# Attention logits by VectorE instead of TensorE, and a shared node tile kept as dense products, in a two-front relational GNN kernel

## The chip, the cores and the metric

The kernel runs on one core of one Trainium2 chip. The metric is device time in microseconds (us) of one execution, median over several runs. A profiled execution gives the trace; its own time is stated beside its span.

## The reference

A graph of 6250 nodes with 256 features and 100000 edges, sorted by destination; each edge has one of 8 relations. Three relational layers are followed by a residual LayerNorm, an attention step and a second residual LayerNorm. Cut to what matters:

```python
for l in range(3):                                   # relational layers
    xr  = einsum('nd,rde->rne', x, W_rel[l])         # 8 products per node
    agg = segment_sum(xr[edge_type, src], dst, N)    # gather by edge, sum by destination
    x   = relu(agg + x @ W_root[l] + bias[l])
x = layernorm(x_in + x)
xt      = (x @ weight).reshape(N, 4, 64)             # attention
alpha_l = einsum('ehd,hd->eh', xt[src], attn_l)      # only edges e < N are used
alpha_r = einsum('ehd,hd->eh', xt[dst], attn_r)
alpha   = softmax(leaky_relu(alpha_l + alpha_r, 0.01))
tmp     = einsum('nh,nhd->nd', alpha[:N], xt[dst[:N]])
out     = layernorm(x + tile(tmp, 4))
```

Everything is float32. `alpha_l` of a node is its normed row times a 256x4 matrix, `weight` folded with `attn_l`; the kernel computes that matrix once (`fold_weights`, columns `D + H` to `D + 2H` of the tile `w1x`).

## The kernel before

**Layers.** Edges are cut in 782 tiles of 128. The first 36 ("hot" ones, of the first few nodes) are handled by counts (`count`, `products`); the other 746 are gathered one by one in each of the three layers. `gather` (L497) has GpSimd issue one indirect DMA per edge tile, 128 rows of 256 floats into a quarter of an `msg` buffer. The pool `mp` has eight such buffers of four tiles, and the hot products and the attention's preparation take buffers from the same pool. `windows` (L514) multiplies the gathered rows with one-hot matrices `oh` (made by VectorE, L481) on TensorE into PSUM, and `add` (L526) has VectorE add the result into a ring `S`, in which the columns of a few node tiles of 128 nodes lie, by relation.

**Two fronts.** The tiles are cut in 188 groups of up to four. Two fronts go down the sorted edges at once and alternate group by group: the upper front (f = 0, ring of 4 node tiles) and the lower one (f = 1, ring of 3). When the last group that touches node tile j of a front is done, `dense` multiplies that tile's `S` with the layer's weights: 2 products with `wo` (L578) and 16 with `wr` (L582), each of which is two float32 passes in the profile. It is a generator: at most six products per group and waiting tile are issued between `windows` and `add`, so they fill in on TensorE. `finish` (L594 to L618) adds the bias, and in layers 0 and 1 applies ReLU and stores the row block for the next layer; in layer 2 it adds the residual and norms the rows to `yt`. `clear` zeroes the columns of the ring on ScalarE (L591).

**The shared tile.** One node tile, number 13, is touched by both fronts. When the lower front is through with it (after group 7) `keep` copies its whole `S` block, 128x2048 floats, to `hold` on ScalarE (L568). After group 181, when the upper front is through, VectorE adds that block to the upper `S` (L825, 128x2048), and one dense product does both.

**Logits.** In layer 2, two groups after a tile is normed, `logits` (L619 to L632) computes its four `alpha_l`: two transposes on TensorE (L549, in `turn`), a copy to SBUF by ScalarE (L552), matmuls with the folded columns (L630) and a copy of 128x4 by VectorE to `altab` (L632). Tile 0 is only transposed, for the attention. From group 164 on `prepare` makes the tables of the attention step between the groups.

**Order.** Within a layer the instructions run on every engine in the order in which the program writes them. Per group: hot products or preparation, loads of rows, `gather`, the one-hot of four groups ahead, `logits` of tiles normed two groups ago, `finish` of the tiles whose products are done, `windows`, the next pieces of `dense`, `add`, transposes of rows (`turn`), then the folding of the ring's end (`fold`, L558 and L560, where a ring wraps) and the queueing of tiles that became ready.

Of the kernel before, what the change touches and what calls it, by code (L numbers as in the profile page):

```python
# [20 lines left out]
P = 128  # L21
# [137 lines left out]
def fast(tc, const, pl, x, xs, src, dst, edge_type, w_rel, w_root, bias, weight,  # L159
# [10 lines left out]
    with ExitStack() as top:  # L170
        tab = top.enter_context(tc.tile_pool(name="tab", bufs=1))
        ident = tab.tile([P, P], F32, name="ident")
        idx = tab.tile([P, CH * P], I32, name="idx")
        key = tab.tile([P, CH * P], F32, name="key")
        pos = tab.tile([1, CH * P], I32, name="pos")
        iota_p = tab.tile([P, 1], F32, name="iota_p")
        eps = tab.tile([P, 1], F32, name="eps")
        bias_b = tab.tile([P, L, D], F32, name="bias_b")
        w1x = tab.tile([P, KC, D + 2 * H], F32, name="w1x")
        altab = tab.tile([P, NT, H], F32, name="altab")  # L180
        al3 = tab.tile([P, 3, NT, H], BF16, name="al3")
        ga = tab.tile([P, NT, H], F32, name="ga")
        hif = tab.tile([P, NT], F32, name="hif")
        dt = tab.tile([P, NT], F32, name="dt")
        yT0 = tab.tile([P, KC, P], F32, name="yT0")


        A = tab.tile([P, NT, HOT * R], F32, name="A")

        psi = top.enter_context(tc.tile_pool(name="psi", bufs=1, space=PSUM))  # L190
        iota = psi.tile([P, max(R * WMAX, NT * R)], F32, name="iota")
        hk = tab.tile([P, pl.TH], F32, name="hk")
        hl = tab.tile([P, pl.TH], F32, name="hl")

        dram = top.enter_context(tc.tile_pool(name="lanes", bufs=1, space=DRAM))
        lane = dram.tile([NT * P], I32, name="lane")
        with tc.tile_pool(name="ps_p", bufs=2, space=PSUM) as ps_p:
            tables(tc, pl, ps_p, src, dst, edge_type, ident, idx, key, pos, iota, iota_p,
                   lane, hk, hl, hif, dt, flag, R, H)
        y = dram.tile([NT * P, D], F32, name="y")  # L200

        with ExitStack() as s:
            wp = s.enter_context(tc.tile_pool(name="wp", bufs=1))
            sp = s.enter_context(tc.tile_pool(name="sp", bufs=1))
            mp = s.enter_context(tc.tile_pool(name="mp", bufs=8))
            op = s.enter_context(tc.tile_pool(name="op", bufs=AHEAD + 2))
            xp = s.enter_context(tc.tile_pool(name="xp", bufs=3))
            hp = s.enter_context(tc.tile_pool(name="hp", bufs=1))
            ps_w = s.enter_context(tc.tile_pool(name="ps_w", bufs=4, space=PSUM))
            ps_d = s.enter_context(tc.tile_pool(name="ps_d", bufs=2, space=PSUM))  # L210
            ps_t = s.enter_context(tc.tile_pool(name="ps_t", bufs=1, space=PSUM))


            S = [sp.tile([P, KR, n * P + PAD], F32, name=f"S{f}") for f, n in enumerate(NS)]

            hold = {j: sp.tile([P, KR, P], F32, name=f"hold{j}") for j in sorted(pl.shared(pl.TM))}

            nc.vector.memset(eps, EPS)
            for t in S:
                nc.scalar.memzero(t)  # L220
            nc.sync.dma_start(bias_b, bias.rearrange("l d -> (l d)").partition_broadcast(P))
            fold_weights(tc, mp, w1x, weight, attn_l, attn_r)

            def load_w(l):
                wr = wp.tile([P, KC, R, D], F32, name="wr")
                wo = wp.tile([P, KC, D], F32, name="wo")
                for k in range(KC):
                    nc.scalar.dma_start(
                        wr[:, k], w_rel[l, :, k * P:(k + 1) * P, :].rearrange("r p e -> p r e"))
                    nc.scalar.dma_start(wo[:, k], w_root[l, k * P:(k + 1) * P, :])  # L230
                return wr, wo

            groups = pl.order()

            ready = {}
            for i, (f, g) in enumerate(groups):
                for j in pl.reach(g):
                    ready[f, j] = i

            with tc.manual_schedule():  # L240
                for l in range(L):
                    wr, wo = load_w(l)
                    opn = layer(
                        tc, pl, l, l == L - 1, groups, ready, S, hold, A, hk, hl, idx, key, pos,
                        iota, ident, wr, wo, bias_b, x, xs, eps, w1x, altab, y,
                        (al3, ga, hif, yT0, lane, dst, iota_p),
                        mp, op, xp, hp, ps_w, ps_d, ps_t, H)

        with tc.manual_schedule():
            attention(tc, pl, opn, A, al3, ga, hif, dt, yT0, iota, ident, eps, w1x, altab, y, out, H)  # L250
# [210 lines left out]
def layer(tc, pl, l, final, groups, ready, S, hold, A, hk, hl, idx, key, pos, iota, ident, wr, wo,  # L461
# [101 lines left out]
        at = (j % NS[f]) * P  # L563
        return S[f][:, :, at:at + P]

    def keep(j):

        i = nc.scalar.copy(hold[j], cols(1, j))  # L568
        tc.add_to_no_dep_group(f"used{l}_1_{j}", i.ins)
        done[1].append(j)  # L570
        clear(1, j)

    def dense(f, j, xT):

        pd = ps_d.tile([P, 512], F32, name="pd")
        s = cols(f, j)
        for k in range(KC):
            nc.tensor.matmul(pd[:, :D], xT[:, k], wo[:, k], start=(k == 0), stop=False)  # L578
            yield
        for k in range(KC):  # L580
            for r in range(R):
                i = nc.tensor.matmul(pd[:, :D], s[:, k * R + r], wr[:, k, r],  # L582
                                     start=False, stop=(k == KC - 1 and r == R - 1))
                tc.add_to_no_dep_group(f"used{l}_{f}_{j}", i.ins)
                if k < KC - 1 or r < R - 1:
                    yield
        done[f].append(j)
        fin.append((f, j, pd))
# [2 lines left out]
        i = nc.scalar.memzero(cols(f, j))  # L591
        tc.add_to_no_dep_group(f"used{l}_{f}_{j}", i.ins)

    def finish(j, pd):  # L594
        n = rows(j)
        nc.vector.tensor_tensor(pd[:, :D], pd[:, :D], bias_b[:, l], ALU.add)  # L596
        if not final:
            h = xp.tile([P, D], F32, name="h", bufs=2)
            nc.scalar.activation(h, pd[:, :D], AF.Relu)  # L599
            nc.sync.dma_start(xs[l + 1][j * P:j * P + n, :], h[:n])  # L600
            return
        xin = xp.tile([P, D], F32, name="xres", bufs=2)
        if n < P:
            nc.vector.memset(xin, 0.0)
        nc.sync.dma_start(xin[:n], x[j * P:j * P + n, :])
        z = xp.tile([P, D], F32, name="h", bufs=2)
        nc.vector.scalar_tensor_tensor(z, pd[:, :D], 0.0, xin, op0=ALU.max, op1=ALU.add)
        st = xp.tile([P, 6], F32, name="st")
        mv = xp.tile([P, 2], F32, name="mv")
        rs = xp.tile([P, 1], F32, name="rs")  # L610
        nc.vector.bn_stats(st, z)
        nc.vector.bn_aggr(mv, st)  # L612
        nc.scalar.activation(rs, mv[:, 1:2], AF.Sqrt, bias=eps)  # L613
        nc.vector.reciprocal(rs, rs)
        yt = xp.tile([P, D], F32, name="yt", bufs=2)
        nc.vector.tensor_scalar(yt, z, mv[:, 0:1], rs, op0=ALU.subtract, op1=ALU.mult)
        nc.sync.dma_start(y[j * P:(j + 1) * P, :], yt)
        return yt  # L618

    def logits(j, yt):  # L620

        if j == 0:
            turn(yt, yT0)
            return
        if prepared:
            opn.append(j)
        yT = turn(yt)
        pt = ps_t.tile([P, 4 * P], F32, name="pt")
        for k in range(KC):
            nc.tensor.matmul(pt[:, :H], yT[:, k], w1x[:, k, D + H:D + 2 * H],  # L630
                             start=(k == 0), stop=(k == KC - 1))
        nc.vector.tensor_copy(altab[:, j], pt[:, :H])  # L632

    def count():

# [140 lines left out]
    prep = prepare() if final else iter(())  # L776
    if final:
        nc.vector.memset(altab, 0.0)
    for i in range(NG + 5):

        ahead = i >= PREP_AT and (i >= NG or groups[i][0] == 1)
# [3 lines left out]
            next(counting, None)  # L785
        if i >= HOT_AT:
            next(hot, None)
        for j in sorted(fetch.get(i, []), reverse=True):
            held[j] = load_rows(j)
        if i < NG:  # L790
# [5 lines left out]
            logits(j, yt)  # L796
        log = [(k, t) for k, t in log if k > i - 2]
        for f, j, pd in fin:
            yt = finish(j, pd)
            clear(f, j)  # L800
            if final:
                log.append((i, (j, yt)))
        fin.clear()
        if i < NG:
# [13 lines left out]
            xTs[j] = turn(held.pop(j))  # L818
        for f, j in sorted((k for k, r in ready.items() if r == i), key=lambda k: -k[1]):
            fold(f, j)  # L820
            if f == 1 and j in late:
                keep(j)
                continue
            if j in hold:
                nc.vector.tensor_tensor(cols(f, j), cols(f, j), hold[j], ALU.add)  # L825
            turned.append(dense(f, j, xTs.pop(j)))
    assert not (turned or fin or log or held or xTs)
    assert next(counting, None) is None and next(hot, 0) == 0 and next(prep, None) is None
    return sorted(opn)
# [544 lines left out]
```

## Time and profile before

| what | value |
|---|---|
| median of 3 runs | 2976.59 us (2976.0 to 2979.49) |
| profiled execution | 2982.89 us, span 2981.1 us |
| mean granted TensorE clock | 0.936 |
| TensorE busy | 2671.0 us (90%) |
| VectorE busy | 1668.5 us (56%) |
| ScalarE busy | 458.6 us (15%) |
| GpSimd busy | 2140.4 us (72%) |
| L497 gathers | 2238, mean 952 ns |
| L549 transposes of `yt`, layer 2 | 98 |
| L630 matmul instructions, layer 2 | 192, mean 266 ns |
| L825 add of the held block | 3, 2291 ns each |

The span runs from the first to the last instruction; the execution's own time also has what lies before and after. Busy time is the share in which an engine executes an instruction; issuing, semaphores and branches don't count. In the views, PE is TensorE, PEld its weight loads, DVE VectorE, ACT ScalarE, POOL GpSimd, SP the engine that only issues DMAs. In a group's row the times after the second bar are the engine's idle time just before these instructions and what ended most of it.

### The profile page before, as it was taken

How to read it: one execution, taken by the hardware profiler on the slowest of the kernel's cores; microseconds unless marked ns; L12 is line 12 of the kernel's file. 1: busy time of each engine (PE TensorE's matmuls, PEld its weight loads, DVE VectorE, ACT ScalarE, POOL GpSimd, SP SyncE). 2: the span in 40 equal slices, each digit the busy share in tenths (PEclk: the TensorE clock that was granted, in tenths of full speed). 3: DMA queues.
4: the chain of work that ended last, by engine and by line, in shares of the span. 5: the costliest groups of instructions: out<-in, count | busy, mean ns of one | idle time of the engine just before them, and what ended most of it. 6: DMA issues, size and time to landing. Idle time of an engine off the chain costs nothing.

```text
span 2981.1 us, 45287 instructions
## 1 busy us (share of the span) xinstructions
PE 2671.0 (90%) x15710; PEld 2428.2 (81%) x15711; DVE 1668.5 (56%) x4094; ACT 458.6 (15%) x602; POOL 2140.4 (72%) x2254
## 2 busy tenths in 40 slices
PE   5999999999877799999988998689999999999985
PEld 4989888888776688988887887678888888888874
DVE  7645677764433455554444443256566655554778
ACT  2111111111001011111111110111111111110114
POOL 6777777777775777777777777577777777777741
PEclk9999999999988899999999997789999999998985
DMA  4444344445433444444444543344444444454534
GB/s 153 125 122 122 119 123 120 120 134 158 146 117 106 122 125 122 125 124 118 120 119 142 170 125 118 117 119 128 130 127 130 123 129 127 133 177 135 165 119 166
DMA packets 203053, 388.97 MB, mean 130 GB/s; under 512 B 42885, under 2 KB 128004, under 8 KB 202820
## 3 DMA queue, kind: packets, MB, share of 16 engines
q0 software_dynamic: 107424, 293.48, 33.6%
q1 hardware_dynamic: 87464, 85.04, 8.8%
q10 hardware_dynamic: 7932, 7.48, 0.8%
q8 instruction: 130, 2.13, 0.3%
q14 instruction: 103, 0.84, 0.1%
HBM read 360.18 MB, written 25.65 MB: 129 GB/s over the span
## 4 chain that ended last, share of the span: by engine, by line
PE 69%; POOL 10%; issue 8%; DVE 6%; DMA 5%; ACT 2%; DVEq 0%; ACTq 0%; POOLq 0%; SPq 0%
PE pw L514 31%; PE pd L582 29%; POOL msg L497 10%; PE pd L578 4%; DMA msg<-x,idx 3%; DVE S L526 3%; PE pd L686 1%; DMA msg<-in_x_dram,idx 1%; PE pt L549 1%; PE pt L630 1%; ACT xT L552 1%; PE pd L657 1%; ACT o L1053 0%; DMA wr<-in_L_gnn_W_rel_dram 0%; DVE oh L481 0%
## 5 line engine op out<-in xcount | busy, mean ns | idle before, releaser
L497 POOL DMA_INDIRECT msg<-x,idx x1492 | 1419.7, 952 | 513.9 <-issue 413.7
L514 PE MATMUL pw<-oh,msg 128*128 128x160 f32 (+22 forms) x8952 | 1305.7, 303 | 202.8 <-DMA msg<-x,idx 99.8
L514 PEld LDWEIGHTS pw<-oh,msg 128*128 128x128 f32 x8952 | 1250.9, 202 | 268.2 <-issue 127.8
L526 DVE TENSOR_TENSOR S<-S,pw 128x320 f32 (+22 forms) x2238 | 905.3, 405 | 998.1 <-PE pd L582 509.0
L582 PE MATMUL pd<-wr,S 128*128 128x256 f32 x4704 | 1108.8, 386 | 1.7 <-DVE S L526 1.4
L582 PEld LDWEIGHTS pd<-wr,S 128*128 128x128 f32 x4704 | 896.3, 194 | 118.0 <-DVE S L526 3.6
L497 POOL DMA_INDIRECT msg<-in_x_dram,idx x746 | 709.2, 951 | 236.1 <-issue 208.4
L481 DVE TENSOR_TENSOR oh<-iota,key 128x640 f32<-128x640 f32 (+23 forms) x564 | 364.2, 647 | 26.5 <-issue 14.8
L591 ACT ACTIVATE S<-S 128x2048 uint32<-128x2048 uint32 x150 | 285.0, 1900 | 0.1
L552 ACT COPY xT<-pt 128x256 f32<-128x256 f32 x195 | 72.3, 371 | 983.6 <-PE pt L549 983.5
L599 ACT ACTIVATE h<-pd 128x256 f32<-128x256 f32 x98 | 37.6, 384 | 933.5 <-DVE pd L596 752.3
L578 PE MATMUL pd<-wo,xT 128*128 128x256 f32 x588 | 170.0, 415 | 3.3 <-ACT h L599 3.3
L596 DVE TENSOR_TENSOR pd<-pd,bias_b 128x256 f32<-128x256 f32 x147 | 63.2, 430 | 172.5 <-PE pd L582 172.5
L578 PEld LDWEIGHTS pd<-wo,xT 128*128 128x128 f32 x588 | 111.2, 207 | 13.3 <-ACT h L599 3.7
L648 DVE TENSOR_SCALAR sel<-iota,hk 128x392 bf16<-128x392 f32 x138 | 80.4, 613 | 0.0
L613 ACT ACTIVATE rs<-mv,eps 128x1 f32<-128x1 f32 x49 | 14.4, 295 | 417.9 <-DVE mv L612 417.9
L686 PE MATMUL pd<-msg,A 128*128 128x256 f32 x294 | 72.5, 390 | 1.5 <-DMA msg<-x 1.5
L686 PEld LDWEIGHTS pd<-msg,A 128*128 128x128 f32 x294 | 56.7, 200 | 8.7 <-issue 1.9
L549 PE MATMUL pt<-ident,xin 128*128 128x128 f32 x294 | 57.6, 278 | 1.4 <-ACT xT L552 1.4
L630 PEld LDWEIGHTS pt<-w1x,xT 128*128 128x128 f32 x192 | 26.6, 201 | 35.2 <-ACT xT L552 35.2
L549 PEld LDWEIGHTS pt<-ident,xin 128*128 128x128 f32 x294 | 41.6, 146 | 12.9 <-ACT xT L552 2.6
L630 PE MATMUL pt<-w1x,xT 128*128 128x4 f32 x192 | 30.8, 266 | 23.5 <-ACT xT L552 23.5
(187 smaller groups left out, 640.0 us busy)
## 6 DMA issues: line engine op xcount, KB each, us to landing
msg<-x,idx POOLq DMA_INDIRECT x1492, 2.7
x<-h SPq DMA_DIRECT2D x96, 128.0 KB
xin<-x SPq DMA_DIRECT2D x96, 128.0 KB
msg<-x SPq DMA_DIRECT2D x24, 512.0 KB
msg<-in_x_dram,idx POOLq DMA_INDIRECT x746, 2.7
y<-yt SPq DMA_DIRECT2D x49, 128.0 KB
wr<-in_L_gnn_W_rel_dram ACTq DMA_DIRECT2D x6, 1024.0 KB
xin<-in_x_dram SPq DMA_DIRECT2D x48, 128.0 KB
```

The source lines that it names most:

```text
L481: nc.vector.tensor_tensor(oh[:, :len(g), :w], iota[:, :w].unsqueeze(1).to_broadcast([P, len(g), w]), key[:, g[0]:g[-1] + 1].unsqueeze(2).t ...
L497: nc.gpsimd.indirect_dma_start(out=msg[:, q, :], out_offset=None, in_=table, in_offset=bass.IndirectOffsetOnAxis(ap=idx[:, t:t + 1], axis=0))
L514: nc.tensor.matmul(pw[:, k * w:(k + 1) * w], msg[:, q, k * P:(k + 1) * P], oh[:, q, :w], start=True, stop=True)
L526: ins = nc.vector.tensor_tensor(o, o, pw.rearrange("p (a b) -> p a b", b=W), ALU.add)
L549: nc.tensor.transpose(pt[:, k * P:(k + 1) * P], t[:, k * P:(k + 1) * P], ident)
L552: nc.scalar.copy(xT.rearrange("p k n -> p (k n)"), pt[:, :D])
L578: nc.tensor.matmul(pd[:, :D], xT[:, k], wo[:, k], start=(k == 0), stop=False)
L582: i = nc.tensor.matmul(pd[:, :D], s[:, k * R + r], wr[:, k, r], start=False, stop=(k == KC - 1 and r == R - 1))
L591: i = nc.scalar.memzero(cols(f, j))
L630: nc.tensor.matmul(pt[:, :H], yT[:, k], w1x[:, k, D + H:D + 2 * H], start=(k == 0), stop=(k == KC - 1))
L648: nc.vector.tensor_scalar(oh, iota[:, :NT * R], float(512 * n), hk[:, t:t + 1], op0=ALU.add, op1=ALU.is_equal)
L686: nc.tensor.matmul(ph[:, :D], A[:, j], t[:, n], start=(n == 0), stop=(j == js[-1]))
```

## The change

Two parts. In layer 2, `logits` no longer uses TensorE and ScalarE: VectorE multiplies the normed rows `yt`, repeated four times, with a tile `wal` that holds the four folded columns as rows on every partition (L627, 128x1024), and sums each 256 products (L628). `spread` makes `wal` once, at group 1 of layer 2, by copying each column 128 times wide and multiplying with the identity. In every layer, the lower front's part of tile 13 is no longer kept as an `S` block: its 16 products with `wr` are computed at once (without those with `wo`), `finish` copies the 128x256 result to `hold`, and the upper front's result gets it added there.

```diff
-            hold = {j: sp.tile([P, KR, P], F32, name=f"hold{j}") for j in sorted(pl.shared(pl.TM))}
+            hold = {j: sp.tile([P, D], F32, name=f"hold{j}") for j in sorted(pl.shared(pl.TM))}
...
-    def keep(j):
-
-        i = nc.scalar.copy(hold[j], cols(1, j))
-        tc.add_to_no_dep_group(f"used{l}_1_{j}", i.ins)
-        done[1].append(j)
-        clear(1, j)
-
     def dense(f, j, xT):
...
-        for k in range(KC):
+        for k in range(KC if xT is not None else 0):
             nc.tensor.matmul(pd[:, :D], xT[:, k], wo[:, k], start=(k == 0), stop=False)
             yield
...
-                                     start=False, stop=(k == KC - 1 and r == R - 1))
+                                     start=(xT is None and k == r == 0), stop=(k == KC - 1 and r == R - 1))
...
-    def finish(j, pd):
+    def finish(f, j, pd):
         n = rows(j)
+        if f == 1 and j in late:
+
+            nc.vector.tensor_copy(hold[j], pd[:, :D])
+            return
+        if j in hold:
+            nc.vector.tensor_tensor(pd[:, :D], pd[:, :D], hold[j], ALU.add)
...
-        yT = turn(yt)
-        pt = ps_t.tile([P, 4 * P], F32, name="pt")
-        for k in range(KC):
-            nc.tensor.matmul(pt[:, :H], yT[:, k], w1x[:, k, D + H:D + 2 * H],
-                             start=(k == 0), stop=(k == KC - 1))
-        nc.vector.tensor_copy(altab[:, j], pt[:, :H])
+        pr = hp.tile([P, H, D], F32, name="pr", bufs=1)
+        nc.vector.tensor_tensor(pr, wal, yt.unsqueeze(1).to_broadcast([P, H, D]), ALU.mult)
+        nc.vector.tensor_reduce(altab[:, j], pr, AX.X, ALU.add)
+
+    def spread():
+
+        for h in range(H):
+            pt = ps_t.tile([P, 4 * P], F32, name="pt")
+            for k in range(KC):
+                t = xp.tile([P, P], F32, name="xres", bufs=2)
+                nc.vector.tensor_copy(t, w1x[:, k, D + H + h:D + H + h + 1].to_broadcast([P, P]))
+                nc.tensor.matmul(pt[:, k * P:(k + 1) * P], t, ident, start=True, stop=True)
+            nc.scalar.copy(wal[:, h], pt[:, :D])
...
+        wal = hp.tile([P, H, D], F32, name="wal")
...
+        if final and i == 1:
+            spread()
...
-            if f == 1 and j in late:
-                keep(j)
-                continue
-            if j in hold:
-                nc.vector.tensor_tensor(cols(f, j), cols(f, j), hold[j], ALU.add)
-            turned.append(dense(f, j, xTs.pop(j)))
+            kept = f == 1 and j in late
+            turned.append(dense(f, j, None if kept else xTs.pop(j)))
```

More of the change, by code (lines that the diff above doesn't have):

```diff
@@ L798, in layer @@
         for f, j, pd in fin:
-            yt = finish(j, pd)
+            yt = finish(f, j, pd)
             clear(f, j)
-            if final:
+            if yt is not None:
                 log.append((i, (j, yt)))
```

## The prediction

> **What bounds the kernel now.** I read the page first. TensorE looks like the bound: busy 90% of the span, and first in the chain that ended last. GpSimd has 72%, but its row L497 shows something odd: a gather takes 952 ns, and nearly all the idle time before it is "issue", a wait for nothing the profile shows.
>
> ```profile
> PE 2671.0 (90%) x15710; PEld 2428.2 (81%) x15711; DVE 1668.5 (56%) x4094; ACT 458.6 (15%) x602; POOL 2140.4 (72%) x2254
> ...
> PE 69%; POOL 10%; issue 8%; DVE 6%; DMA 5%; ACT 2%; DVEq 0%; ACTq 0%; POOLq 0%; SPq 0%
> ...
> L497 POOL DMA_INDIRECT msg<-x,idx x1492 | 1419.7, 952 | 513.9 <-issue 413.7
> ```
>
> Next the timeline of GpSimd alone. An undisturbed gather starts every 1.25 us (0.945 busy, 0.30 issue). A layer has 746 of them: 932.5 us. From the first gather's start to the last one's end the three layers measure as the rows of busy time by stage below say (first column the stretch, then its length): 936.2, 935.7 and 956.8 us. **GpSimd paces layers 0 and 1 completely; only layer 2, the one changed most, has slack: about 21 us.**
>
> ```profile
> 11.10:947.30 936.20, 853.85 (x5032) 772.04 (x5032) 551.18 (x1397) 143.38 (x162) 709.23 (x746) 0.96 0.43 128
> 968.00:1903.70 935.70, 844.99 (x4873) 775.13 (x4873) 451.65 (x1012) 123.41 (x145) 708.49 (x746) 0.93 0.43 127
> 1924.10:2880.90 956.80, 880.39 (x5294) 801.63 (x5294) 572.43 (x1380) 138.21 (x193) 711.13 (x746) 0.96 0.46 137
> ```
>
> The waits of GpSimd in layer 2 say where the 21 us went (total, times, longest). The time beyond 0.30 each, summed over the timeline's gaps, is 18.4 us; layers 0 and 1 have nearly none once they are under way.
>
> ```profile
> POOL msg L497 <- PE pw L514: 25.1, 38, 3.6
> ...
> POOL msg L497 <- DMA msg<-x,idx: 7.4, 19, 1.9
> POOL msg L497 <- PE pt L549: 6.2, 12, 2.6
> ...
> POOL msg L497 <- DVE ga L756: 1.3, 1, 1.3
> ```
>
> By place: 3.6 us between 2235 and 2313 (TensorE is up to 35 us behind and the eight msg buffers are full), 6.1 at 2587 to 2651 (the hot products also take msg buffers), 3.1 at 2774 and 5.9 at 2850 to 2876 (the attention's preparation takes them too).
>
> Last, what lengthens a gather. Two pairs from the timeline (start, length):
>
> ```profile
> 2342.17 0.69 DVE L558 TENSOR_TENSOR S<-S 128x512 f32<-128x512 f32 x1
> 2342.27 1.41 POOL L497 DMA_INDIRECT msg<-x,idx  x1 [0.30 <-issue]
> ...
> 2853.25 2.29 DVE L825 TENSOR_TENSOR S<-S,hold 128x2048 f32<-128x2048 f32 x1
> 2853.38 3.07 POOL L497 DMA_INDIRECT msg<-x,idx  x1 [0.30 <-issue]
> ```
>
> A gather that starts inside a VectorE tensor_tensor with both inputs in SBUF ends late, by about the time to that operation's end less 0.13 us: 0.46 of 0.59 us left in the first pair, 2.13 of 2.16 in the second. All three L825 behave so (1.69, 1.75, 2.13 us). Of the 39 L558, 23 have a gather starting inside and cost 5.16 us together, 0.13 each. The L526 adds, with one input in PSUM, leave the gathers over them at 946 ns.
>
> [...]
>
> **The change, part by part.**
>
> *Logits off TensorE.* For 48 node tiles of layer 2 go two transposes, ScalarE's copy, four weight-load and matmul pairs (L630), and VectorE's copy L632. On TensorE one costs about 1.5 us (2308.7 to 2310.2 in the timeline: 0.38 transposing, 0.46 waiting for ScalarE, 0.61 multiplying): 72 us in all. That can't come off the time, since gathers pace the layer. It buys only the waits for late TensorE: 3.6 + 6.1 + 3.1 = 12.8 us. Layer 1, which has no logits, shows TensorE at most 12 us behind at the same groups and no such waits, so I take all 12.8 (bounds 8 and 14). I keep the 5.9 at the end: there the preparation and two dense products hold the buffers. At the very end L632 waits for TensorE until 2899.1 with the last tile's bias add behind it, though that tile's products ended at 2897.7: 1.4 us gained.
>
> *Logits onto VectorE.* A product 128x1024 (L627 of the new file) and a reduction to four (L628), 48 times. Length: L558 takes 692 ns for 512 and L825 2291 for 2048, so 1.04 ns an element and 1.22 us for 1024. The reduction: 681 ns for 512 contiguous elements (L356) gives about 1.21; if it ran like L756's strided one (854 for 392), 2.2. Together 2.4 us, 117 us in layer 2, raising VectorE there from 572 to 690 of 957 us. It delays the finish and the S adds that stand behind it, and TensorE waits for those; TensorE's lag and its 70 freed us cover this. Without that cover it would cost up to 0.5 us a tile.
>
> **The product has both inputs in SBUF, so it stalls gathers; this decides.** Taking a random phase in the 1.25 us cycle, a product of 1.22 us leaves (1.22 − 0.13)² / (2 × 1.25) = 0.48 us a tile. The same formula for L558 gives 0.564²/2.5 = 0.127 us, measured 0.13. About 46 of the 48 fall while gathers run: **22 us added**. Bounds: none [...], and 46 × 1.09 = 50 us (if each were met at the worst phase).
>
> *spread().* Eight column copies, eight matmuls and four ScalarE copies, once, at group 1 of layer 2: some 5 us of TensorE while it waits for gathers anyway (5.7 us idle at 1932 to 1938). [...] I take 0; without the cover 5.
>
> *The shared tile (13), in each layer.* Added: 32 matmul instructions, 7.2 us by the last tile's row (7.17 for x32), near group 7. In layer 0 the least distance of a gather from waiting on its buffer is 9.4 us around group 92, so 7.2 still fits; layer 1 has 21. Cost 0; without that cover 7 a layer. ScalarE loses a 1.9 us copy nobody waits for. L825, 2.29 us, becomes an add of 128x256 with PSUM (0.43, like L596). Its stall of a gather (1.7 to 2.1 us) goes, but right after it TensorE, not the gather, is late (products of tiles 14 and 13), so I count 0; bounds 0 to 2 a layer. The copy to hold (0.4 us) hides in VectorE's idle time.
>
> No DMA is added, removed or moved; SP's queue keeps its order.
>
> **Sum:** + 22.0 − 12.8 − 1.4 = **+7.8 us**. The profiled execution was 2982.9 us (span 2981.1), some 6 us above the median 2976.6. So about 2990.7 for its like, and **2984.4 us** for the median. Own range, from 8 to 14 us of waits saved, a spread of the stalls of some 4 us, and 0 to 3 of new waits at the end: 2976 to 2993.
>
> **Rivals.**
> 1. *No stall, faster.* [...] only the gains stay: −14.2, 2962.4 us. [...] Against: all L825 and all the L558 that were met. It decides from below 14.2/46 = 0.31 us a tile; with L825's stalls gone too, nothing below 2955 is possible, since the gathers' own 932.5 us a layer stay.
> 2. *More stall, or VectorE binding.* VectorE runs the products after a one-hot whose time follows the gathers, so the phase may lock: +50 − 14.2, 3012 us. Or product, reduction, finish and adds in one group exceed its 5.0 us, and TensorE falls behind waiting for S: 0.5 us on 46 tiles, +23 on top of the forecast, 3007. For it: the DVE chain of one group can reach 0.7 + 2.4 + 1.8 + 2.0. Against: products and finishes rarely share a group.
> 3. *TensorE-bound throughout.* −72 us, 2905. Excluded by the gathers' floor unless their cycle shortens; nothing suggests it.
> 4. *The change does not do what it says:* the extra dense product or new prep waits shift the end by several us either way.
>
> **How the numbers follow.** A measurement here can tell about 0.2%, 6 us, from no change. Forecast 0.62, rival 1 0.15, rival 2 0.18, rivals 3 and 4 0.05. The forecast's mean of +7.8 puts 0.37 of its 0.62 beyond +6 and 0.25 within; rival 1 gives 0.13 faster, 0.02 within; rival 2 0.18 slower; the rest 0.02 faster, 0.03 slower. Faster 0.15, same 0.27, slower 0.58. The range reaches to rival 1's 2962 and most of rival 2's: 2962 to 3004.
>
> **What would show it.** Right: layer 2's gathers from first to last about 965 us; mean gather in layer 2 near 0.98; gathers of 1.1 to 2.0 us exactly where a product runs; no waits for PE before group 164; TensorE idle for gathers as in layer 1; the 3 long gathers at the layers' ends gone. Wrong: gathers under the product at 0.946 (rival 1), or mean stalls near 1 us, or TensorE waiting for S in place of gathers (rival 2), or waits for PE near group 60 still there.

## The result, and the profile after

The changed kernel takes 2990.15 us (median of 13 runs, 2984.1 to 2998.37), the kernel before 2976.59 in as many runs beside it (2971.55 to 2986.63): ratio 1.0041, 95% interval 1.0032 to 1.005. By this ratio it is 12.2 us slower (9.5 to 14.9; the two medians lie 13.6 us apart), where the forecast was +7.8. A later measurement gave 1.0047 (1.0031 to 1.0062). The first profiled execution took 2987.91 us, span 2986.1.

The page of the changed kernel first: engines, shares of the chain that ended last, and three groups (busy us and mean ns after the first bar, idle time before them after the second).

```profile
PE 2670.7 (89%) x15534; PEld 2428.8 (81%) x15535; DVE 1770.2 (59%) x4153; ACT 436.2 (15%) x555; POOL 2154.6 (72%) x2254
...
PE 65%; POOL 10%; DVE 9%; issue 9%; DMA 5%; ACT 1%; DVEq 0%; POOLq 0%; ACTq 0%
...
L497 POOL DMA_INDIRECT msg<-x,idx x1492 | 1435.0, 962 | 502.6 <-issue 414.0
...
L628 DVE TENSOR_REDUCE altab<-pr 128x4 f32<-128x1024 f32 x48 | 58.6, 1220 | 1.6
L627 DVE TENSOR_TENSOR pr<-wal,yt 128x1024 f32<-128x1024 f32 x48 | 58.3, 1215 | 0.0
```

Product and reduction take 1.215 and 1.220 us, as priced. The mean of the gathers in this row, the 1492 of layers 1 and 2, rose from 952 to 962 ns, though no gather was added: they are 15.3 us longer in all. (Layer 0 gathers from the input and has a row of its own, so the 952 ns of the table of before hold for these 1492, not for all 2238.)

Busy time by stage, for the gathers of the three layers as before (stretch, length, then PE, PEld, DVE, ACT, POOL):

```profile
11.00:946.10 935.10, 860.68 (x5057) 777.40 (x5057) 549.19 (x1397) 141.38 (x161) 708.15 (x746) 0.96 0.43 128
967.80:1902.10 934.30, 851.19 (x4894) 780.57 (x4895) 450.14 (x1012) 121.02 (x143) 707.04 (x746) 0.93 0.43 127
1923.80:2883.70 959.90, 864.77 (x5073) 790.35 (x5073) 672.11 (x1434) 120.14 (x149) 727.92 (x746) 0.94 0.46 137
```

Layers 0 and 1 stayed within 1.4 us of what they were: they are 1.1 and 1.4 us shorter, since the long gather under the add of the held block is gone, and the way from each one's last gather to the next layer's first is 1.0 and 1.3 us longer. In layer 2 the gathers need 3.1 us more, and GpSimd's busy time rose by 16.8 us, from 711.13 to 727.92. Its waits in that layer went the other way (total, times, longest, 0.30 of each being the ordinary gap):

```profile
POOL msg L497 <- PE pw L514: 12.0, 33, 2.2
POOL msg L497 <- DMA msg<-x,idx: 10.9, 29, 2.4
POOL msg L497 <- DVE ga L762: 1.3, 1, 1.3
```

Beyond 0.30 each, the gaps sum to 5.0 us instead of 18.7. Waits saved were paid back as longer gathers. Three of these in the timeline (start, length):

```profile
2199.10 1.22 DVE L627 TENSOR_TENSOR pr<-wal,yt 128x1024 f32<-128x1024 f32 x1
2200.02 1.11 POOL L497 DMA_INDIRECT msg<-x,idx  x1 [0.30 <-issue]
...
2249.15 1.21 DVE L627 TENSOR_TENSOR pr<-wal,yt 128x1024 f32<-128x1024 f32 x1
2249.70 1.48 POOL L497 DMA_INDIRECT msg<-x,idx  x1 [0.30 <-issue]
...
2262.10 1.21 DVE L627 TENSOR_TENSOR pr<-wal,yt 128x1024 f32<-128x1024 f32 x1
2262.73 1.41 POOL L497 DMA_INDIRECT msg<-x,idx  x1 [0.30 <-issue]
```

The rule of the prediction gives each from the two starts: 2249.15 + 1.21 − 2249.70 − 0.13 = 0.53 us, and 1.48 − 0.945 is 0.535. Of the 46 products in this stretch all 46 have a gather starting inside, for 19.3 us in all (0.42 each). In the 36 of them with more than 0.25 us left at the gather's start, the rule misses by at most 0.01 us.

The span's growth of 5.0 us by place: layer 2's gathers start 0.3 earlier, run 3.1 longer, the last windows follow the last gather 2.2 sooner, and from the last windows' end to the program's end it is 96.5 instead of 92.1 us, 4.4 more. From the last gather's end it is 102.4 instead of 100.2, 2.2 more, where the prediction had 1.4 less. TensorE at that place and the window adds just ahead, the kernel before:

```profile
2889.53 0.99 DVE L526 TENSOR_TENSOR S<-S,pw 128x64 f32 x4
2890.57 7.17 PE L582 MATMUL pd<-wr,S 128*128 128x256 f32 x32 [0.61 <-DVE S L526]
```

and the changed kernel, with VectorE's queue ahead of it:

```profile
2884.15 1.21 DVE L627 TENSOR_TENSOR pr<-wal,yt 128x1024 f32<-128x1024 f32 x1
2885.40 1.22 DVE L628 TENSOR_REDUCE altab<-pr 128x4 f32<-128x1024 f32 x1
2886.54 0.98 DVE L526 TENSOR_TENSOR S<-S,pw 128x64 f32 x4
...
2890.40 0.42 DVE L594 TENSOR_TENSOR pd<-pd,hold 128x256 f32<-128x256 f32 x1
...
2893.32 0.99 DVE L526 TENSOR_TENSOR S<-S,pw 128x64 f32 x4
...
2894.36 9.94 PE L575 MATMUL pd<-wr,S 128*128 128x256 f32 x32 [3.23 <-DVE S L526]
```

In the last groups VectorE has almost no gap: tile 14's product and reduction stand ahead of the preparation, the hold add (L594), the finish of tile 13 and the last window adds (L526). TensorE needs those adds for the first node tile's products. They start 9.6 us after the last gather's end (2893.32 − 2883.70) instead of 8.6, so VectorE's queue costs 1.0 us here. TensorE idles 3.23 us instead of 0.61; the other 1.6 us of this is only that it reaches this place sooner. Then the same 32 products (L575, formerly L582) take 9.94 us instead of 7.17. The windows view of that stretch says why: the figure after POOL's, the granted clock, is 0.50 in the first 3 us, 0.55 in the next 3, and then 1.00. (The first two rows are of the time ahead of the wait.)

```profile
2888.00:2889.70 1.70, 1.70 (x17) 1.68 (x15) 1.60 (x3) 0.00 (x0) 0.00 (x0) 1.00 0.00 0
2889.80:2891.10 1.30, 1.30 (x4) 0.52 (x2) 1.27 (x4) 0.00 (x0) 0.00 (x0) 0.50 0.00 0
2894.30:2897.30 3.00, 2.94 (x7) 2.40 (x8) 2.93 (x5) 0.26 (x1) 0.00 (x0) 0.50 0.27 85
2897.30:2900.30 3.00, 3.00 (x9) 2.38 (x9) 0.19 (x1) 0.00 (x0) 0.00 (x0) 0.55 0.00 0
2900.30:2904.40 4.10, 4.00 (x19) 3.18 (x17) 0.06 (x1) 0.00 (x0) 0.00 (x0) 1.00 0.00 0
```

The clock fell between the first two rows, at 2889.75, 1.4 us before the wait of 3.23 us began, and the longest idle time of TensorE in the 10 us before that was 0.62 us. So this wait did not bring the clock down; what did is not shown. The kernel before has a half clock too, a little earlier and with TensorE at work in it, but it was over before the 32 products:

```profile
2883.50:2886.80 3.30, 3.30 (x9) 2.46 (x8) 3.07 (x6) 0.00 (x0) 0.00 (x0) 0.50 0.00 0
```

### The profile page after: what moved, and what is told of

It reads as the page before. It is cut to its first block, busy times and chain, and to the rows that moved or that the text cites. A ratio compares the mean times of both kernels' runs of the same rounds, so it can differ in the third digit from the quotient of the medians.

```text
span 2986.1 us, 45003 instructions
## 1 busy us (share of the span) xinstructions
PE 2670.7 (89%) x15534; PEld 2428.8 (81%) x15535; DVE 1770.2 (59%) x4153; ACT 436.2 (15%) x555; POOL 2154.6 (72%) x2254
## 4 chain that ended last, share of the span: by engine, by line
PE 65%; POOL 10%; DVE 9%; issue 9%; DMA 5%; ACT 1%; DVEq 0%; POOLq 0%; ACTq 0%
PE pw L514 29%; PE pd L575 29%; POOL msg L497 10%; DVE S L526 4%; PE pd L571 4%; DMA msg<-x,idx 4%; PE pd L692 1%; DMA msg<-in_x_dram,idx 1%; DVE oh L481 1%; PE pd L663 1%; PE pt L549 1%; DVE pr L627 0%; DVE st L1035 0%; DVE z L1023 0%; DMA wr<-in_L_gnn_W_rel_dram 0%
## 5 line engine op out<-in xcount | busy, mean ns | idle before, releaser
L497 POOL DMA_INDIRECT msg<-x,idx x1492 | 1435.0, 962 | 502.6 <-issue 414.0
L514 PE MATMUL pw<-oh,msg 128*128 128x160 f32 (+22 forms) x8952 | 1320.1, 305 | 231.9 <-DMA msg<-x,idx 107.3
L514 PEld LDWEIGHTS pw<-oh,msg 128*128 128x128 f32 x8952 | 1266.0, 204 | 306.9 <-issue 126.5
L526 DVE TENSOR_TENSOR S<-S,pw 128x320 f32 (+22 forms) x2238 | 904.9, 404 | 949.8 <-PE pd L575 482.2
L575 PE MATMUL pd<-wr,S 128*128 128x256 f32 x4800 | 1128.9, 385 | 4.3 <-DVE S L526 4.1
L575 PEld LDWEIGHTS pd<-wr,S 128*128 128x128 f32 x4800 | 912.0, 194 | 124.5 <-DVE S L526 6.3
L552 ACT COPY xT<-pt 128x256 f32<-128x256 f32 x147 | 54.4, 370 | 894.0 <-PE pt L549 893.9
L628 DVE TENSOR_REDUCE altab<-pr 128x4 f32<-128x1024 f32 x48 | 58.6, 1220 | 1.6
L627 DVE TENSOR_TENSOR pr<-wal,yt 128x1024 f32<-128x1024 f32 x48 | 58.3, 1215 | 0.0
```

The costliest lines, as they stand in the source:

```text
L497: nc.gpsimd.indirect_dma_start(out=msg[:, q, :], out_offset=None, in_=table, in_offset=bass.IndirectOffsetOnAxis(ap=idx[:, t:t + 1], axis=0))
L514: nc.tensor.matmul(pw[:, k * w:(k + 1) * w], msg[:, q, k * P:(k + 1) * P], oh[:, q, :w], start=True, stop=True)
L526: ins = nc.vector.tensor_tensor(o, o, pw.rearrange("p (a b) -> p a b", b=W), ALU.add)
L628: nc.vector.tensor_reduce(altab[:, j], pr, AX.X, ALU.add)
```

## The experiments

Theory A is the forecast's: gathers pace the kernel, and the product with two SBUF inputs lengthens them. Rival B: VectorE's 117 us of added work cost the time. Theory C, added after the result: the end grew because VectorE's queue delays the last window adds. Each ratio below is to the kernel before, run beside it on the same chip. The first four experiments happened to run on a chip where the kernel before takes 3605.08 us instead of 2977, so their times answer another question than the one put.

**1. The shared tile alone.** The second part of the change in the kernel before; logits stay on TensorE. Of its edit against the kernel before, two places:

```diff
-            if f == 1 and j in late:
-                keep(j)
-                continue
-            if j in hold:
-                nc.vector.tensor_tensor(cols(f, j), cols(f, j), hold[j], ALU.add)
-            turned.append(dense(f, j, xTs.pop(j)))
+            kept = f == 1 and j in late
+            turned.append(dense(f, j, None if kept else xTs.pop(j)))
...
+        if j in hold:
+            nc.vector.tensor_tensor(pd[:, :D], pd[:, :D], hold[j], ALU.add)
```

> Only the shared tile is changed; the logits stay on TensorE as before. Theory A (gathers pace layers 0 and 1; a product of two SBUF operands stalls them in layer 2): layers 0 and 1 keep their length within 1 us, layer 2 has no product, so no stall; but TensorE is 35 us behind there around group 60 and the 7.2 us of new dense work turn into up to 6 us of gather waits: 0 to +6 us against the kernel before, some 2979. Rival B (it is VectorE's added work, not the stall, that costs): +0.5 us, 2977. Rival C (the lost time comes from the tail after the last gather, through the add of the held block): +3 to +5 us, in the tail alone.

Measured: 3604.28 us, ratio 0.9989 (0.997 to 1.0008): no difference. But on this chip the gathers do not pace. The profile of this run (clock, and the group of gathers):

```profile
core 0: 3622.2 us, clock 0.875
```

```profile
L497 POOL DMA_INDIRECT msg<-x,idx x1492 | 1415.2, 949 | 964.8 <-issue 386.8
```

A gather takes what it took (a mean of 949 ns), but GpSimd's idle time before these is 964.8 us instead of 513.9. Beyond the ordinary gap it waits 184 to 236 us a layer. Some six tenths of this ended when TensorE freed a buffer; most of the rest, 61 to 71 us a layer, the profile puts to no engine of this core. TensorE is busy for 80% of this span, not 90%, so it is late without being full. Why this chip runs so was not settled.

**2. The normed rows through PSUM.** The product then has one input in SBUF and one in PSUM; VectorE's work is the same.

```diff
+        yp = ps_t.tile([P, 4 * P], F32, name="pt")
+        nc.scalar.copy(yp[:, :D], yt)
-        nc.vector.tensor_tensor(pr, wal, yt.unsqueeze(1).to_broadcast([P, H, D]), ALU.mult)
+        nc.vector.tensor_tensor(pr, wal, yp[:, :D].unsqueeze(1).to_broadcast([P, H, D]), ALU.mult)
```

> The changed kernel, but ScalarE first copies the normed row block to PSUM and the product reads it there: the same VectorE work with one SBUF operand instead of two. Theory A: the gathers under the product stay at 0.95 us, the lengthening of layer 2's gathers falls from 22.5 to about 3 us, layer 2's gathers take about 941 us instead of 960, and the time falls by some 17 to 20 us against the changed kernel, to about 2972, under the kernel before. Rival B (VectorE's work costs): no change against the changed kernel, 2990. Rival C (tail): no change, 2990.

Measured on the slow-paced chip: 3587.61 us, ratio 0.9941 (0.9917 to 0.9965). The lengthening of layer 2's gathers was 2.0 us in all, none of it under the product. Repeated in experiment 5.

**3. and 4. The product twice, the reduction twice.** The line is issued two times per tile; the result is the same.

```diff
         nc.vector.tensor_tensor(pr, wal, yt.unsqueeze(1).to_broadcast([P, H, D]), ALU.mult)
+        nc.vector.tensor_tensor(pr, wal, yt.unsqueeze(1).to_broadcast([P, H, D]), ALU.mult)
```

```diff
         nc.vector.tensor_reduce(altab[:, j], pr, AX.X, ALU.add)
+        nc.vector.tensor_reduce(altab[:, j], pr, AX.X, ALU.add)
```

> The changed kernel with the 128x1024 product issued twice in a row, same result. Theory A: the second product stalls gathers too, 10 to 20 us more lengthening in layer 2, plus 2 to 4 us in the tail: 3002 to 3014. Rival B: 1.2 us more VectorE work per tile, the same as a doubled reduction: +6 us, 2996. Rival C: +2 to +4 us, all in the tail.

> The changed kernel with the reduction issued twice in a row, same result: as much more VectorE time as with a doubled product, but one operand only. Theory A: no gather is lengthened, layer 2's gathers stay at 960 us; only the tail grows, 1 to 4 us: 2991 to 2994. Rival B: the same as the doubled product, +6 us. Rival C: +2 to +4 us, all in the tail.

Measured: 3585.35 us, 0.9938 (0.9916 to 0.996), and 3578.07 us, 0.9922 (0.989 to 0.9954). Both are *faster* than the kernel before, and so is number 2, while number 1, with the logits on TensorE, is not. That fits a chip where TensorE's side is late throughout and taking the logits off it helps; the changed kernel itself was not run there. Neither the stalls nor 58 us more of VectorE can be seen in these times. For the stall itself the traces still speak: 17.9 us under the product with the reduction doubled and none under the reductions, of which the lines ahead of the result had shown nothing; with the product doubled 16.7 us under the first and only 0.8 under the second. The timeline of that run shows why the second is nearly free (its L628 is the second product):

```profile
2546.77 1.22 DVE L627 TENSOR_TENSOR pr<-wal,yt 128x1024 f32<-128x1024 f32 x1
2546.88 1.93 POOL L497 DMA_INDIRECT msg<-x,idx  x1 [0.30 <-issue]
2548.01 1.22 DVE L628 TENSOR_TENSOR pr<-wal,yt 128x1024 f32<-128x1024 f32 x1
2549.11 0.95 POOL L497 DMA_INDIRECT msg<-x,idx  x1 [0.30 <-issue]
```

The gather waits for the first product's end (1.93 us). The second product begins while that gather is under way and adds nothing: by the rule of the prediction the first product alone gives 0.945 + 0.98 = 1.93 us. The next gather starts 0.12 us before the second product's end and takes 0.95 us. What was held up here is the gather that *started* under a product with more than 0.13 us left.

**5. The normed rows through PSUM, on a chip where the gathers pace.** The edit of number 2.

> The changed kernel with the normed rows copied to PSUM by ScalarE, so that the product of logits reads one input from SBUF and one from PSUM; the same VectorE work, nothing left out. The first time this edit ran, on a chip on which GpSimd does not set the pace, it only showed that the product no longer lengthens gathers; what this is worth in time needs a chip on which the kernel before takes about 2977 us and the gathers pace. Theory A (gathers pace, the two-SBUF product stalls them by 0.42 us on 46 tiles): gathers of layer 2 from first to last about 941 us instead of 960, lengthening below 5 us, and the time about 19 us below the changed kernel: ratio to the kernel before about 0.998 (0.997 to 0.999), +4 us of tail included. Rival B (VectorE's 117 us of added work cost, not the stall): time as the changed kernel's, ratio 1.003 to 1.005, with new waits of TensorE for VectorE in layer 2.

Measured: 2977.96 us, the kernel before 2981.76 beside it; ratio 0.9991 (0.9982 to 0.9999). Layer 2's gathers, and one product with the gathers around it (L629 is the product here):

```profile
1926.40:2874.40 948.00, 869.23 (x5073) 790.82 (x5073) 671.38 (x1434) 135.59 (x196) 710.91 (x746) 0.94 0.47 138
```

```profile
2223.16 0.95 POOL L497 DMA_INDIRECT msg<-x,idx  x1 [0.30 <-issue]
2223.51 1.21 DVE L629 TENSOR_TENSOR pr<-wal,pt 128x1024 f32<-128x1024 f32 x1
2224.42 0.94 POOL L497 DMA_INDIRECT msg<-x,idx  x1 [0.30 <-issue]
```

VectorE is as busy as in the changed kernel (671 us), GpSimd is back at 711, and the gather under the product takes 0.94 us. Rival B expected no gain here and falls. The stage is 12 us shorter than with the product from SBUF, not the 19 expected: 4.9 us of waits came back near its end (9.9 instead of 5.0), and a single gather was 949 ns long instead of 946 in the whole execution, 746 × 0.003 = 2.2 us a layer.

**6. Logits behind their own group's adds.** In the last eight groups `logits` is issued after `add`.

```diff
+        due = [t for k, t in log if k <= i - 2]
+        if i < NG - 8:
+            for j, yt in due:
+                logits(j, yt)
...
             add(i, wins, vals)
+        if i >= NG - 8:
+            for j, yt in due:
+                logits(j, yt)
```

> The changed kernel with one thing moved: in the last eight groups of layer 2 and in the steps after the last gather the product and reduction of a tile are issued behind the finish and the window adds instead of ahead of them; same instructions, nothing left out. Theory C (the end of layer 2 grew by 4.4 us because product, reduction and hold add stand ahead of the last window adds on VectorE, so that the first node tile's dense product starts 3.8 us late and then runs in 9.9 us instead of 7.2): the stretch from the last gather's end to the end of the program falls from 102.4 to 97-100 us, the L575 group of tile 0 takes about 7.2 us again, ratio to the kernel before 1.0015 to 1.003 against 1.004 of the changed kernel. If the tail is set elsewhere (the attention's gathers or SP's queue): tail unchanged within 1 us, ratio 1.003 to 1.005. A loss is possible as well, if the last tile's logits then end the chain: tail +1 to +2 us.

Measured: 2994.07 us, ratio 1.0049 (1.0032 to 1.0065); from the last windows' end it is 97.3 us, and from the last gather's end 102.3, as in the changed kernel. No gain: behind one group's adds is still ahead of the next group's finish and adds, and TensorE's wait grew to 4.67 us. The edit was no test of theory C.

**7. Both.** Numbers 2 and 6 together.

> Both edits together: normed rows through PSUM for the product, and logits behind the window adds in the last eight groups; nothing left out. If theory A and theory C both hold the gains add: gathers of layer 2 about 941 us, tail 97-100 us, 21 to 24 us below the changed kernel: ratio to the kernel before 0.995 to 0.998, which would beat both kernels. Rival B: no gain from the PSUM copy, ratio 1.001 to 1.004.

Measured: 2981.01 us, ratio 0.9998 (0.9989 to 1.0006), where 0.995 to 0.998 was expected. Layer 2's gathers took 947.4 us, as in number 5, but the end grew to 100.4 us: the transposes of tile 0, which the attention waits for, now stood behind a product that held their PSUM buffer (6.7 us of waiting for L629).

**8. The shared tile alone, where the gathers pace.** The edit of number 1.

> The kernel before with only the second part of the change: the shared tile 13 as a dense product per layer, logits still on TensorE; nothing left out. The prediction priced this part at zero. Theory A: the same time as the kernel before within 0.1%, gathers of layers 0 and 1 from first to last 935 us each, the three long gathers under L825 gone, layer 2 about 955 us. Rival (the dense product's 7.2 us of TensorE per layer come out at each layer's end, and some of the 8 us of the measured slowdown that the two profiled executions do not show come from it): 7 to 20 us slower, ratio 1.002 to 1.007, with windows of layers 0 and 1 ending later than 953.4 and 1909.3 us.

Measured: 2985.41 us, ratio 1.0015 (1.0008 to 1.0022), 4.5 us slower where 0 was expected. Its three stages are 937.4, 935.7 and 955.9 us, and the long gathers under L825 are gone. Here too a single gather was 949 ns long, which is 2.2 us a layer; without that the stages are 935.2, 933.5 and 953.7, none longer than before. Against that, the ways between the layers are 1.8 and 1.7 us longer and the end 0.6; the windows of layers 0 and 1 end at 956.7 and 1913.7 us, later than in the kernel before (953.4 and 1909.3), as the rival had said; 2.2 and 4.4 us of that are the longer single gathers. So the profile, without the 6.6 us of longer single gathers, shows no net cost of the part, while its runs show one of 2.4 to 6.6 us. Which length the unprofiled runs had is not known; whether this part costs anything stays open.

**9. Through PSUM, and the logits of the last groups kept back** until the last window adds are out. This is the edit that theory C asked for. Beside number 2's lines:

```diff
         due = [t for k, t in log if k <= i - 2]
+        if NG - 3 <= i <= NG:
+            kept_back += due
+        else:
+            for j, yt in due:
+                logits(j, yt)
...
             add(i, wins, vals)
+        if i == NG:
+            for j, yt in kept_back:
+                logits(j, yt)
```

> The changed kernel with the product reading the normed rows from PSUM and, in the last three groups of layer 2, the logits kept back until the last window adds are issued; nothing left out. The edit late_logits did not take the product of tile 14 from ahead of the last finish and adds: it moved it behind the adds of its own group, which is still ahead of the next group's. This one does. Theory C in this form (product and reduction of tile 14, 2.4 us, delay the last finish and window adds, TensorE idles 3.2 us or more and then runs the 32 products of tile 0 in 9 to 10 us instead of 7.2): from the last windows' end to the program's end 91 to 93 us instead of 96.6, the wait ahead of tile 0's products at most 1.3 us and these back at 7.2 us. With theory A: gathers of layer 2 about 946 to 948 us. Ratio to the kernel before 0.996 to 0.998, about 16 to 20 us below the changed kernel, and faster than both. If the tail is set elsewhere: 95.5 to 96.5 us, and the ratio 0.999.

Measured: 2968.92 us (20 runs), the kernel before 2976.78; ratio 0.9969 (0.9962 to 0.9976). It beats both kernels: by the ratio 9.2 us under the kernel before (7.1 to 11.3), and some 22 under the changed one. By stage, and its end:

```profile
11.30:945.40 934.10, 862.82 (x5056) 778.61 (x5056) 549.56 (x1397) 141.38 (x161) 706.75 (x746) 0.96 0.44 129
967.40:1900.80 933.40, 849.97 (x4892) 778.52 (x4893) 450.13 (x1012) 121.01 (x143) 706.17 (x746) 0.93 0.44 127
1923.70:2864.30 940.60, 857.51 (x5073) 780.56 (x5073) 672.47 (x1434) 135.24 (x195) 707.94 (x746) 0.95 0.47 139
```

```profile
2872.57 8.64 PE L575 MATMUL pd<-wr,S 128*128 128x256 f32 x32 [2.30 <-DVE S L526]
```

All three layers are now within 9 us of the gathers' own 932.5; for layer 2, 946 to 948 had been expected. The end is 93.8 us from the last windows, against 96.5 and an expected 91 to 93. From the last gather's end it is 98.8 against 102.4 (and 100.2 before): the last window adds start 7.2 us after that gather instead of 9.6, sooner by the 2.4 us of product and reduction. TensorE still idles 2.30 us, since preparation and the finish of tile 13 stand ahead of the adds, and 3 us of the products run at half clock.

**10. The changed kernel again**, on the same chip as 9.

> The changed kernel as it is, for its time beside the other edits on one chip and for a second profile; nothing left out. Theory A: ratio to the kernel before 1.003 to 1.005 again; gathers of layer 2 about 960 us, 46 of 46 products met by a gather, about 19 us of lengthening there; tail 96 to 97 us from the last windows' end. Single undisturbed gathers come at 946 or at 949 ns in every profile so far, one value for a whole execution: if it is the second, the span is 6.6 us longer than the 2986 us of the first profile, about 2992.7. If that length belongs to the code, it is 946 again and the span 2986 within 2 us.

Measured: 2991.45 us, ratio 1.0047 (1.0031 to 1.0062). The profile repeats in kind: 46 of 46 products met, 20.8 us; layer 2's gathers 964.3 us; 96.2 us at the end; single gathers of 946 ns. Its span of 2989.7 us fits neither of the two that had been expected; the 3.6 us above the first profile lie in layer 2's gathers.

**11. The kernel before against itself**, same chip.

> The kernel before as it is, against itself; nothing left out. It tells how large a difference identical code can show: ratio 1.000, and by how much the interval can be off. Theory (length of a single gather is a property of the execution): either 946 ns and a span of about 2981 us less the run-to-run spread of 3 us, or 949 ns and a span about 6.6 us longer for otherwise the same stretches. Rival (it belongs to the code): 946 ns always. The stretches from the last windows' end to the end should be 92 us as before, with the products of tile 0 in 7.2 us.

Measured: 2976.93 us, ratio 0.9999 (0.9991 to 1.0007). Span 2981.2, layer 2's gathers 956.3 us, 91.8 us at the end, 7.17 us for the 32 products.

**12. Logits kept back, product from SBUF.** Of number 9 only the second edit, to split its gain.

> The changed kernel with only the second of the two edits of psum_end: logits kept back in the last three groups, the product still with both inputs from SBUF; nothing left out. It splits the 22 us between the changed kernel and psum_end into the part of the tail and the part of the stall. Theories A and C: gathers of layer 2 about 960 to 963 us with 45 products met and about 19 us of lengthening, the tail from the last windows' end 93 to 94 us, about 3 to 6 us below the changed kernel: ratio to the kernel before 1.002 to 1.0035, so that 16 to 19 us are left to the stall. If keeping the logits back is what brought psum_end its gain: ratio below 1.000 and gathers of layer 2 near 945 us.

Measured: 2986.5 us, the kernel before 2975.7 beside it; ratio 1.0035 (1.0022 to 1.0047). All 46 products met, 19.7 us; 94.1 us at the end, 99.1 from the last gather instead of 102.4. Layer 2's gathers took 967.3 us, 4 more than expected, because 11.0 us of waits are left, 5.7 of them in one group of the preparation. Against number 9 only the place of one product input differs: 1.0035 − 0.9969 = 0.0066, or 20 us. The two ran on different chips, each beside the kernel before; by the two intervals it is 15 to 24 us.

## Why the prediction was right

Its direction, its mechanism and most of its terms held; one term had the wrong sign, and the sum came out too low: +7.8 us lies below the measured 9.5 to 14.9.

- *What paces.* Right. Layers 0 and 1, with no logits, kept their lengths, and 72 us of TensorE work taken out of layer 2 bought only waits: those ahead of 2850 us fell from 12.8 us to none, as the forecast said (in the second pair of profiles from 11.5 to none).
- *The stall.* Right. Forecast 0.48 us on 46 tiles, 22.0 us; in the traces 19.3, 20.8 and 19.7 us; by the comparison of 12 with 9 about 20 us. Every product was met, as one of 1.22 us in a cycle of 1.25 nearly must be. The mean gather of layer 2 is 727.92 / 746 = 0.976 us (0.98 said), and the layer's gathers take 960 and 964 us (965 said). As a difference this term is +3.1 and +8.0 us where 22.0 − 12.8 = 9.2 was forecast: in the first pair the stall is 2.7 us smaller, the waits saved 0.9 larger, and the long gather under L825, whose loss was counted as 0, gives 2.1 back; what is left is small.
- *Waits of the preparation kept at 5.9.* Right in size: 5.0 and 8.0 us. They vary by some us from edit to edit.
- *Layers 0 and 1, the dense product of the shared tile at 0.* Right for the changed kernel, whose windows of the two layers end at 953.3 and 1909.2 us against 953.4 and 1909.3. Number 8 leaves up to 6.6 us open.
- *The end, −1.4.* Here a step failed. The 1.4 us did come: in the kernel before VectorE's bias add starts 1.5 us after the first tile's products end, in the changed one at once. But counted from the last gather these products end 3.7 us later. The failed sentence is "TensorE's lag and its 70 freed us cover this": at the last groups nothing lies behind which VectorE's extra 2.4 us and the hold add could hide. Their adds start 1.0 us later, and the products themselves take 2.8 us longer at half clock, for which the prediction had no term and whose start is not explained. The prediction had put "0 to 3 of new waits at the end" in its range only. The term is +2.2 us in the first pair of profiles and +2.0 in the second, instead of −1.4.
- *Rivals.* Rival 2 did not show: the stalls stayed below half a microsecond a tile, and VectorE's load by itself cost nothing while gathers ran (number 5), only at the end. Rival 1 (no stall, −14.2) is what number 9 builds: −9.2 by its runs, −18.1 by the two profiled spans (2963.1 and, beside it, 2981.2); why these differ is open, as below. Its floor of 2955 us does not follow from the prediction's own figures: the three stages lie 31.2 us above 3 × 932.5, which gives 2945. Rival 3 is what the first four runs show a piece of: on a chip where TensorE's side is late everywhere, kernels with the logits on VectorE gain 0.6 to 0.8%.

The pieces make +5.0 us in the first pair of profiles and +8.5 in the second (layer 2's gathers +8.0, their end to the last windows −2.4, the end +4.4, an earlier start of layer 2 −1.5), around the forecast's +7.8. That the first pair comes so near is in part luck: its gathers lost 6.1 us less than forecast and its end 3.6 us more. The ratios of the runs give +12.2 and +14.0. The profiled executions of the kernel before were 6 us above its median both times (2982.89 against 2976.59, 2982.96 against 2976.93), those of the changed kernel 2 us below and level. So 5.5 to 7 us of the measured loss stand in no profile. Their cause is open.

The logits part alone was not tried. By the sizes of the tiles it needs 7 KB a partition more than the changed kernel, whose `hold` takes 1 KB instead of 8; whether that fits is not shown.

## What to carry to other kernels

Before moving work from the busiest engine, ask which instruction stream paces the stage: here 90% busy TensorE had slack, and GpSimd at 72% had none. When VectorE works under a stream of gathers from GpSimd that paces the kernel, try an input from PSUM for an operation like this product: with both inputs in SBUF the 128x1024 product cost the gathers 0.42 us per tile, and with one in PSUM the gather under it took 0.94 us. Cover that holds over a stage ends at its last groups, so work that nobody waits for belongs behind the last adds (here these started 7.2 us after the last gather instead of 9.6).

## What was unexpected of the hardware

- TensorE's clock fell to half (0.50) in the changed kernel with no wait above 0.62 us in the 10 us before. The 32 products of the first tile took 7.17 us after waits of 0.61 and 1.08 us, 8.64 and 8.86 after 2.30 and 2.29, 9.94 after 3.23, and 9.13 to 9.72 after 3.86 to 4.67. But the wait need not be the cause: in the profiles the clock fell 1.4 us before it (the changed kernel), 1.8 us into it (the changed kernel again) or 1.1 us after its end (number 12).
- The product from SBUF held up gathers that started under it (0.42 us each on 46 tiles of the changed kernel); in number 3 a product that began 1.13 us after the gather added nothing to its 1.93 us. And it is not always the gather that gives way. Six gathers in four profiles (numbers 3, 4, 6 and 12) start at most 0.03 us after the product; they keep their length, and the product takes 1.26 to 1.29 us instead of 1.22. One of number 12:

```profile
2282.39 1.27 DVE L627 TENSOR_TENSOR pr<-wal,yt 128x1024 f32<-128x1024 f32 x1
2282.41 0.95 POOL L497 DMA_INDIRECT msg<-x,idx  x1 [0.30 <-issue]
```

  What in the gather waits for the product is not shown.
- An undisturbed gather lasts 946 ns in a whole execution or 949 in a whole execution. The same code had both, on two chips (experiments 2 and 5), and one chip had both, with different codes (experiments 5 and 6), so neither alone sets it. 2238 × 0.003 us is 6.6 us of span, more than many an edit. What sets it is not known.
- The same kernel took 2976 to 2982 us (medians) on four occasions and 3605 on one chip, with single gathers equally long.
